# A graph network layer on one core: early phase reordered, node term by products, three VectorE operands moved to PSUM

## The chip, the cores and the metric

The kernel runs on one core of one Trainium2 chip. The metric is the device time of one execution in microseconds; the figure quoted is the median of six executions.

## The reference

There are 12,500 nodes with 96 features (`x`) and 412,500 directed edges, sorted by destination, with 4 attributes each. `_mlp` is a linear layer, ReLU and a normalisation over all rows (batch statistics).

```python
node_feat = _mlp(x, W_node, ...)                     # 12500 x 96
edge_feat = _mlp(edge_attr, W_edge, ...)             # 412500 x 96
message = _mlp(concat([x[row], x[col], edge_feat]), W_msg, ...)
agg = segment_sum(message, col, num_segments=12500)
out = layernorm(x + agg + node_feat)                 # per node, over 96 features
```

The batch normalisation of the messages is linear, so it can be applied after the segment sum; the kernel does so.

## The kernel before

**Tiling.** The edges are cut into tiles of 128, four tiles make a group (`GT`), four groups a block (`BG`): 806 groups, 202 blocks. As the edges are sorted, a block touches a short run of destination nodes; it starts at the node number `base[b]`.

**Tables.** `table` (line 144) multiplies all nodes by a 96x96 part of `W_msg` and writes the rows to DRAM, once for the source part (`p_tab`) and once for the destination part (`q_tab`). Its input `xp` is `x` transposed, loaded in seven pieces (line 98), on the queues of SP and ScalarE in turn. The tables' copies out of PSUM are shared by VectorE and ScalarE (lines 156, 158).

**Gathers.** Rows of `p_tab` are fetched for each tile of 128 edges by one indirect DMA that GpSimd issues (line 166). The first 26 blocks (the spilled ones; the first three of them take rows of `x` itself) are gathered ahead, during the early phase: `blocks` (line 171) gathers one block of 16 tiles into one of two `stage` buffers and writes it to DRAM (`spill`, line 177) from SP's queue. Each `next(store)` puts one such block into the program at that place: two during the first table, four during and after the second, three in `nodes`, the rest in `edge_norm`. The gathers stand in GpSimd's queue in block order and wait only for a free `stage` buffer, that is for the store two blocks before; the stores stand in SP's queue among its other DMAs, so a store can wait behind another DMA, and a DMA behind a store that waits for its gathers. After that, 28 groups are gathered into a ring (`pg`).

**Early phase, in order.** Tables; the check of the node windows (`rel`, line 209, subtracts the block's base node from every edge's destination; lines 213 to 223 reduce it to a flag); `places` (line 225: the same subtraction with edges in a linear layout, stored to DRAM as `rel_d`); `nodes` (line 245): `relu(x W_node + b)` into `agg`, its statistics, then on VectorE `xp = agg * a + xp` (line 260) and on ScalarE `xp = xp + c` (line 261) in ten pieces, then 98 products of `xp` with a centring matrix (line 266), which give `x + node_feat` less its mean over the features, copied (line 270) and stored (line 273) as `y0_d`; a memset of `agg`, which from there on is the sum per node; `edge_norm` (line 277): the edge layer for all edges, for its statistics alone: products (294), ReLU on ScalarE (298), `bn_stats` on VectorE (300).

**Main loop** (`fast`, from line 495, an order written out by hand for all engines, spilled blocks interleaved with the others: about one in eight). For each group `k`:

- `linear` (452): four products `z` of the edge features and one-hot places (`left`) with a matrix `rhs` that holds `w_e`, rows of `q_tab` and a bias. `z` has two buffers of one PSUM bank each, taken in turn.
- `message`: for even groups, `is_equal` (461) of `rel` against the constant `iota` gives the one-hot places of two groups in `h`; `hs = z + pg` (465), VectorE; `h = relu(hs)` (466), ScalarE.
- `sums` (477): `h` transposed times `h`, which gives sums per node and the statistics.
- per block, `edges` (437) makes the edge features of the next block; after group 2's message `prepare` writes them to `left`, half by ScalarE (444) and half by VectorE (445); `add` (490, 491) adds a block's sums.

In iteration `k` TensorE is given `linear(k+1)` and then `sums(k-1)`. When `hs(k)` is done, the ring slot of group `k` is free and GpSimd may gather the group that comes 28 later.

**Final phase** (from line 698): sums per node times a matrix made from the messages' normalisation, plus `y0_d`, layernorm, output.

Of the kernel before, what the change touches and what calls it, by code (L numbers as in the profile page):

```python
# [22 lines left out]
P = 128  # L23
# [53 lines left out]
def gnn(ctx, tc, t):  # L77
# [15 lines left out]
    ring = rpool.enter_context(tc.tile_pool(name="ring", bufs=RING))  # L93
    xp = xpool.enter_context(tc.tile_pool(name="x", bufs=1)).tile([C, XW], F32, name="xp")
    nc.scalar.dma_start(w_msg, t["L0_gnn_W_msg"].rearrange("(s k) f -> k s f", k=C))
    for i in range(0, NB, CH):
        part = slice(COL[i], COL[i + CH] if i + CH < NB else XW)
        (nc.scalar if i // CH % 2 else nc.sync).dma_start(xp[:, part], t["xp"][:, part])
    nc.scalar.dma_start(src, t["src"])

    ident = const.tile([P, P], F32, name="ident")
    make_identity(nc, ident)
# [12 lines left out]
    nc.vector.memset(step[:, 1, :], 1.0)  # L115
    nc.vector.memset(wide, 0.0)
    nc.vector.memset(we, 0.0)

    center = const.tile([C, C], F32, name="center")
# [3 lines left out]
    base = const.tile([1, NBL], I32, name="base")  # L123
    mstat = const.tile([C, 2], F32, name="mstat")
    vec = const.tile([C, len(_VECS)], F32, name="vec")
    v = {name[7:]: vec[:, i:i + 1] for i, name in enumerate(_VECS)}
# [66 lines left out]
    nc.sync.dma_start(base, t["base"])  # L193
# [9 lines left out]
    with tc.tile_pool(name="win", bufs=1) as win, tc.tile_pool(name="win_ps", bufs=2, space=PSUM) as ps:  # L203
        dsti = win.tile([P, NGP, GT], I32, name="dsti")
        nc.sync.dma_start(dsti, t["dst"].rearrange("p (g t) -> p g t", t=GT))
        basei = win.tile([P, NBL], I32, name="basei")
        nc.sync.dma_start(basei, t["base"].to_broadcast([P, NBL]))
        by_block = "p (b g) t -> p b (g t)"
        nc.vector.tensor_tensor(rel.rearrange(by_block, g=BG), dsti.rearrange(by_block, g=BG),
                                basei.unsqueeze(2).to_broadcast([P, NBL, BG * GT]), op=OP.subtract)  # L210
# [12 lines left out]
        nc.vector.tensor_scalar(flag, most, 0.0, None, op0=OP.is_gt)  # L223

    def places():

        with tc.tile_pool(name="lin", bufs=2) as work, tc.tile_pool(name="lin1", bufs=1) as one:
            first = one.tile([P, RW], I32, name="first")
            nc.sync.dma_start(first, t["first"])
            rows = rel_d.rearrange("o (p g e) -> (o p) g e", g=RW, e=GE)  # L230
            parts = [slice(i, min(i + 2, RW)) for i in range(0, RW, 2)]
            lins = []
            for i in range(len(parts) + 1):
                if i < len(parts):
                    n = parts[i].stop - parts[i].start
                    lins.append(work.tile([P, n, GE], I32, name="lin"))
                    nc.sync.dma_start(lins[i], t["dlin"][:, parts[i], :])
                    rlin = work.tile([P, n, GE], F32, name="rlin")
                    nc.vector.tensor_tensor(rlin, lins[i], first[:, parts[i]].unsqueeze(2).to_broadcast([P, n, GE]),
                                            op=OP.subtract)  # L240
                    lins[i] = rlin
                if i:
                    nc.sync.dma_start(rows[:, parts[i - 1], :], lins[i - 1])

    def nodes():

        with tc.tile_pool(name="nd", bufs=1) as one, tc.tile_pool(name="nd_ps", bufs=2, space=PSUM) as ps:
            stats = one.tile([C, -(-N // GE), 6], F32, name="nstats")
            for i, c in enumerate(range(0, N, GE)):
                n = min(GE, N - c)  # L250
                pn = ps.tile([C, GE], F32, name="pn", bufs=4)
                nc.tensor.matmul(pn[:, :n], w_node, xp[:, c:c + n], start=True, stop=True)
                nc.scalar.activation(agg[:C, c:c + n], pn[:, :n], AF.Relu, bias=v["b_node"], scale=1.0)
                nc.vector.bn_stats(stats[:, i, :], agg[:C, c:c + n])
            aggr = one.tile([C, 2], F32, name="naggr")
            nc.vector.bn_aggr(aggr, stats.rearrange("p a b -> p (a b)"))
            a_n, c_n = norm(aggr, v["g_node"], v["beta_node"], "node")
            for c in range(0, N, N // 10):
                x, y = agg[:C, c:c + N // 10], xp[:, c:c + N // 10]
                nc.vector.scalar_tensor_tensor(y, x, a_n, y, op0=OP.mult, op1=OP.add)  # L260
                nc.scalar.activation(y, y, AF.Identity, bias=c_n, scale=1.0)
            for i in range(0, NB, NBY):
                n = min(NBY, NB - i)
                py = ps.tile([P, 2, GE], F32, name="py0")
                for g in range(n):
                    nc.tensor.matmul(py[:, g // NBK, g % NBK * C:(g % NBK + 1) * C],
                                     xp[:, COL[i + g]:COL[i + g] + P], center, start=True, stop=True)
                y0 = one.tile([P, 2, NBK * C], F32, name="y0s", bufs=2)
# [62 lines left out]
    def fast(ring):  # L331
# [3 lines left out]
        with tc.manual_schedule(engines={ET.SP, ET.Pool}):  # L335
# [33 lines left out]
        with tc.tile_pool(name="fix", bufs=1) as fix, tc.tile_pool(name="msg", bufs=2) as work, \  # L369
# [85 lines left out]
            def message(k):  # L455
# [4 lines left out]
                if i % 2 == 0:  # L460
                    nc.vector.tensor_tensor(  # L461
                        h[:, :, :, C + 1:C + 1 + WN], rel[:, g:g + 2, :].unsqueeze(3).to_broadcast([P, 2, GT, WN]),
                        iota[:, i:i + 2, :].unsqueeze(2).to_broadcast([P, 2, GT, WN]), op=OP.is_equal)
                hs = work.tile([P, GT, C], F32, name="hs", bufs=3)
                nc.vector.tensor_add(hs[:, :n, :], z[:, :n, :], pg[:, :n, :])  # L465
                nc.scalar.activation(h[:, i % 2, :n, :C], hs[:, :n, :], AF.Relu)  # L466
# [229 lines left out]


    with tc.tile_pool(name="fin", bufs=2) as work, tc.tile_pool(name="fin_ps", bufs=2, space=PSUM) as ps:
        a_m, c_m = norm(mstat, v["g_msg"], v["beta_msg"], "msg")
        l = const.tile([C, C + 1], F32, name="l")  # L700
        nc.vector.tensor_scalar(l[:, :C], ident[:C, :C], a_m, None, op0=OP.mult)  # L701
        nc.vector.tensor_copy(l[:, C:C + 1], c_m)  # L702
        pd = ps.tile([C + 1, C], F32, name="pd", bufs=1)
        nc.tensor.matmul(pd, l, center, start=True, stop=True)  # L704
        d = const.tile([C + 1, C], F32, name="dm")
        nc.vector.tensor_copy(d, pd)  # L706

        out = t["out"]
        for i in range(0, NB, NBY):
# [58 lines left out]
```

## Time and profile before

| | |
|---|---|
| median of six executions | 5490.99 us (5481.06 to 5501.54) |
| profiled execution | 5504.1 us, span 5502.4 us |
| PE busy | 3509.8 us (64%), 16705 matmuls |
| PE weight loads busy | 2653.2 us (48%) |
| VectorE busy | 1717.5 us (31%) |
| ScalarE busy | 1132.7 us (21%) |
| GpSimd busy | 3053.4 us (55%) |
| mean granted TensorE clock | 0.667 |
| early phase (to the first message) | 0 to 1071.5 us |
| main loop | 1071.5 to 5436.6 us |
| final phase | 5436.6 to 5502.4 us |

No engine is busy for more than about two thirds of the span, so the time is in the waits between them. Matmul rows are issues whose ends are modelled: that a product is done is told by the start of the instruction that waits for it.

### The profile page before, as it was taken

To read this page: it belongs to the slowest core of one execution; us is meant where nothing else is said; L and a number is where in the kernel's file an instruction comes from. 1 tells how busy PE (TensorE), PEld (TensorE's weight loads), DVE (VectorE), ACT (ScalarE), POOL (GpSimd) and SP (SyncE) were. 2 spreads that over 40 slices of the span, in tenths; PEclk is the share of its full clock that TensorE was granted. 3 is DMA by queue.
4 is the path that set the end of the run, shared out by engine and by line. 5 is a ranking of instruction groups with operands and counts; after the bars stand their busy time and mean duration, and the time that the engine had idled before them with its cause. 6 is when DMAs were issued, how large, how long until landed. Compare 5 with 4: busy or idle time off the path is not lost. (4 is left out here: it accounts for less than half of the span.)

```text
span 5502.4 us, 48307 instructions
## 1 busy us (share of the span) xinstructions
PE 3509.8 (64%) x16705; PEld 2653.2 (48%) x16705; DVE 1717.5 (31%) x2837; ACT 1132.7 (21%) x1417; POOL 3053.4 (55%) x3231
## 2 busy tenths in 40 slices
PE   5556652666666666766665766766666666665677
PEld 5333320455555555545544555544444545555457
DVE  1345551722222222222222222222222222222235
ACT  0224441411111111111111111111111111111112
POOL 5454456155565555655566655666556666555650
PEclk9755555566666766666666666677667667666777
DMA  5332321111111111111111111111111111111112
GB/s 162 109 97 62 70 64 43 34 30 37 38 43 37 42 42 42 44 36 41 43 42 43 37 42 42 43 42 44 36 42 43 41 45 36 41 42 42 45 38 73
DMA packets 154615, 270.89 MB, mean 49 GB/s; under 512 B 83665, under 2 KB 84178, under 8 KB 153356
## 3 DMA queue, kind: packets, MB, share of 16 engines
q0 software_dynamic: 103136, 158.62, 12.0%
q1 hardware_dynamic: 48138, 98.39, 6.2%
q10 hardware_dynamic: 3088, 10.71, 0.6%
q8 instruction: 134, 2.20, 0.2%
q14 instruction: 119, 0.97, 0.1%
HBM read 225.88 MB, written 41.60 MB: 49 GB/s over the span
## 5 line engine op out<-in xcount | busy, mean ns | idle before, releaser
L166 POOL DMA_INDIRECT pg<-p_tab,src x2807 | 2656.6, 946 | 1893.5 <-DVE hs L465 1073.3
L452 PE MATMUL z<-rhs,left 128*128 128x96 f32 x6446 | 1232.4, 347 | 857.0 <-issue 701.8
L452 PEld LDWEIGHTS z<-rhs,left 128*128 128x128 f32 x6446 | 1115.0, 257 | 1182.1 <-issue 905.6
L477 PE MATMUL pa<-h 128*97 128x128 f32 x6446 | 1236.4, 335 | 462.2 <-issue 458.1
L477 PEld LDWEIGHTS pa<-h 128*97 128x97 f32 x6446 | 1032.1, 214 | 516.2 <-issue 515.1
L466 ACT ACTIVATE h<-hs 128x384 f32<-128x384 f32 x806 | 416.6, 523 | 3544.7 <-DVE hs L465 2452.8
L465 DVE TENSOR_TENSOR hs<-z,pg 128x384 f32<-128x384 f32 x702 | 383.1, 554 | 2402.1 <-remote 1304.2
L437 PE MATMUL pr<-ea,we 6*127 6x512 f32 x1404 | 542.7, 927 | 124.2 <-issue 110.3
L445 DVE TENSOR_SCALAR left<-pr 31x2048 f32<-31x2048 f32 x202 | 462.9, 2292 | 486.7 <-ACT left L444 258.7
L294 PE MATMUL pr<-ea,wide 10*128 10x512 f32 x1212 | 403.9, 1074 | 315.8 <-issue 214.2
L166 POOL DMA_INDIRECT stage<-p_tab,src x368 | 350.2, 952 | 381.2 <-DMA spill<-stage 248.3
L300 DVE BATCH_NORM_STATS2 estats<-r 128x6 f32<-128x512 f32 x606 | 365.4, 677 | 354.3 <-issue 227.4
L294 PEld LDWEIGHTS pr<-ea,wide 10*128 10x128 f32 x1212 | 202.5, 321 | 515.9 <-issue 333.2
L298 ACT ACTIVATE r<-pr 128x1024 f32<-128x1024 f32 x303 | 295.5, 1024 | 479.9 <-remote 342.2
L444 ACT ACTIVATE left<-pr 96x2048 f32<-96x2048 f32 x202 | 373.7, 1850 | 15.5 <-PE pr L437 15.5
L437 PEld LDWEIGHTS pr<-ea,we 6*127 6x127 f32 x1404 | 163.4, 254 | 341.5 <-issue 331.2
L461 DVE TENSOR_TENSOR h<-rel,iota 128x248 f32<-128x248 f32 x403 | 163.8, 407 | 0.0
L154 PE MATMUL pt<-w_msg,xp 96*128 96x96 f32 x392 | 88.5, 421 | 64.9 <-issue 35.7
L465 DVE TENSOR_TENSOR hs<-z,pb 128x384 f32<-128x384 f32 x104 | 57.1, 554 | 219.6 <-PE z L452 91.1
L154 PEld LDWEIGHTS pt<-w_msg,xp 96*128 96x128 f32 x392 | 85.3, 330 | 67.9 <-issue 47.8
L491 DVE TENSOR_TENSOR gram<-pa,gram 97x388 f32<-97x388 f32 x202 | 111.4, 551 | 0.0
L490 DVE TENSOR_TENSOR agg<-pa,agg 97x62 f32 x404 | 90.1, 223 | 14.1 <-PE pa L477 1.0
(106 smaller groups left out, 650.8 us busy)
## 6 DMA issues: line engine op xcount, KB each, us to landing
pg<-p_tab,src POOLq DMA_INDIRECT x2807
spill<-stage SPq DMA_DIRECT2D x26, 768.0 KB
pb<-spill SPq DMA_DIRECT2D x26, 768.0 KB
ea<-in_ea SPq DMA_DIRECT2D x75, 160.0 KB
rhs<-q_tab SPq DMA_DIRECT2D x404, 23.2 KB
ea<-in_ea SPq DMA_DIRECT2D x352, 20.0 KB
stage<-p_tab,src POOLq DMA_INDIRECT x368
q_tab<-trow SPq DMA_DIRECT2D x7, 672.0 KB
```

Of the source, the lines that this page charges most:

```text
L154: nc.tensor.matmul(pt[:, g, :], xp[:, k:k + P], w, start=True, stop=True)
L166: nc.gpsimd.indirect_dma_start(out=pg[:, i, :], out_offset=None, in_=tab[:, :], in_offset=bass.IndirectOffsetOnAxis(ap=idx[:, k:k + 1], ax ...
L294: nc.tensor.matmul(pr[:, k % 2, :], wide[Q * i:Q * i + 2 * EK, :], ea[Q * i:Q * i + 2 * EK, b % J, :], start=True, stop=True)
L298: nc.scalar.activation(r, pr, AF.Relu)
L300: nc.vector.bn_stats(stats[:, (k - o) % NS, (k - o) // NS, :], r[:, 1 - o, :])
L437: nc.tensor.matmul(prs[s][:C + WN, i, :], we[Q * i:Q * i + EK + 1, :], block[s][Q * i:Q * i + EK + 1, :], start=True, stop=True)
L444: nc.scalar.activation(x[:C, :n, :], pr[:C, :n, :], AF.Relu)
L445: nc.vector.tensor_scalar(x[C:C + WN, :n, :], pr[C:C + WN, :n, :], 0.0, None, op0=OP.is_equal)
L452: nc.tensor.matmul(zs[k][:, i, :], left[s % 2][:KR, g % BG, i * P:(i + 1) * P], rhs[:KR, s % RB, g % BG, :], start=True, stop=True)
L465: nc.vector.tensor_add(hs[:, :n, :], z[:, :n, :], pg[:, :n, :])
L466: nc.scalar.activation(h[:, i % 2, :n, :C], hs[:, :n, :], AF.Relu)
L477: nc.tensor.matmul(pas[s][:, g % BG, :C + 1 + WN], h[:r, i, :C + 1], h[:r, i, :C + 1 + WN], start=i == 0, stop=i == n - 1)
```

## The change

- **Loads in turn.** Four pieces of `xp` are loaded at first; each further piece is issued after a piece of the first table, on the queue of that table's store, and the load of the 1.6 MB index array `src` after the fourth. ScalarE's queue is put in program order for that stretch. `base` is loaded early.
- **Node features by products.** The scaling of lines 260 and 261 is gone. `a` and `c` go into a 97x96 matrix `d` (a diagonal and a row, times the centring matrix), and each tile of `y0` is the sum of two products in PSUM: `xp` with `center`, `agg` with `d`. `agg` has a row of ones for `c`, so it is set to 1 at the start; the memset to 0 at the end of `nodes` stays. Every second copy of `y0` goes to ScalarE. The final phase calls the same new function in place of its own lines.
- **Operands in PSUM.** The subtraction for `rel` takes the bases from PSUM (made there by a product with a row of ones; the broadcast load of 101 KB is gone); the one of `places` takes `first` from PSUM; `is_equal` takes its node numbers from a copy of `iota` in the unused end of the first of the two `z` banks. The two `z` buffers are now two fixed tiles.
- **Stores placed anew.** One more `next(store)` after `places`, and four in `nodes` (at its tiles 0, 3, 7, 11) instead of three (0, 4, 10).

```diff
-    for i in range(0, NB, CH):
+    def load_x(i):
         part = slice(COL[i], COL[i + CH] if i + CH < NB else XW)
         (nc.scalar if i // CH % 2 else nc.sync).dma_start(xp[:, part], t["xp"][:, part])
-    nc.scalar.dma_start(src, t["src"])
+    for i in range(0, 4 * CH, CH):
+        load_x(i)
...
+    nc.vector.memset(agg, 1.0)
...
+    def scaled(aggr, gamma, beta, name, ps):
+        a, c = norm(aggr, gamma, beta, name)
+        l = const.tile([C, C + 1], F32, name=f"l_{name}")
+        nc.vector.tensor_scalar(l[:, :C], ident[:C, :C], a, None, op0=OP.mult)
+        nc.vector.tensor_copy(l[:, C:C + 1], c)
+        nc.tensor.matmul(ps[:C + 1, :C], l, center, start=True, stop=True)
+        d = const.tile([C + 1, C], F32, name=f"d_{name}")
+        nc.vector.tensor_copy(d, ps[:C + 1, :C])
+        return d
...
-    with tc.manual_schedule(engines={ET.SP, ET.Pool}):
+    with tc.manual_schedule(engines={ET.SP, ET.Pool, ET.Activation}):
...
             for i, _ in enumerate(table(p_tab, ...)):
+                if (i + 4) * CH < NB:
+                    load_x((i + 4) * CH)
+                if i == 3:
+                    nc.scalar.dma_start(src, t["src"])
                 if i in (2, 5):
                     next(store)
...
-        nc.sync.dma_start(basei, t["base"].to_broadcast([P, NBL]))
+        nc.vector.tensor_copy(basef, base)
+        nc.tensor.matmul(pb, ones, basef, start=True, stop=True)
...
-                                basei.unsqueeze(2).to_broadcast([P, NBL, BG * GT]), op=OP.subtract)
+                                pb.unsqueeze(2).to_broadcast([P, NBL, BG * GT]), op=OP.subtract)
...
+            first = ps.tile([P, RW], F32, name="first")
+            nc.vector.tensor_copy(first, firsti)
...
-            a_n, c_n = norm(aggr, v["g_node"], v["beta_node"], "node")
-            for c in range(0, N, N // 10):
-                x, y = agg[:C, c:c + N // 10], xp[:, c:c + N // 10]
-                nc.vector.scalar_tensor_tensor(y, x, a_n, y, op0=OP.mult, op1=OP.add)
-                nc.scalar.activation(y, y, AF.Identity, bias=c_n, scale=1.0)
+            d = scaled(aggr, v["g_node"], v["beta_node"], "node", ps.tile([P, GE], F32, name="pn", bufs=4))
...
-                    nc.tensor.matmul(py[...], xp[:, COL[i + g]:COL[i + g] + P], center, start=True, stop=True)
+                    nc.tensor.matmul(to, xp[:, at], center, start=True, stop=False)
+                    nc.tensor.matmul(to, agg[:, at], d, start=False, stop=True)
...
-                if n == NBY:
+                if n == NBY and i // NBY % 2:
+                    nc.scalar.activation(y0, py[:, :, :NBK * C], AF.Copy)
+                elif n == NBY:
                     nc.vector.tensor_copy(y0, py[:, :, :NBK * C])
...
             places()
+            next(store)
             for i, _ in enumerate(nodes()):
-                if i in (0, 4, 10):
+                if i in (0, 3, 7, 11):
                     next(store)
...
+            zb = [ps.tile([P, GE], F32, name=f"z{i}", bufs=1) for i in range(2)]
+            nodes_of = zb[0][:, GT * C:GT * C + BG * WN].rearrange("p (k w) -> p k w", w=WN)
+            nc.vector.tensor_copy(nodes_of, iota)
...
-                zs[k] = ps.tile([P, GT, C], F32, name="z")
+                zs[k] = zb[k % 2][:, :GT * C].rearrange("p (t c) -> p t c", c=C)
...
-                        iota[:, i:i + 2, :].unsqueeze(2).to_broadcast([P, 2, GT, WN]), op=OP.is_equal)
+                        nodes_of[:, i:i + 2, :].unsqueeze(2).to_broadcast([P, 2, GT, WN]), op=OP.is_equal)
```

More of the change, by code (lines that the diff above doesn't have):

```diff
@@ L117, in gnn @@
     nc.vector.memset(we, 0.0)
+    ones = const.tile([1, P], F32, name="ones")
+    nc.vector.memset(ones, 1.0)
     center = const.tile([C, C], F32, name="center")
@@ L121, in gnn @@
     agg = const.tile([C + 1, WT], F32, name="agg")
+    nc.vector.memset(agg, 1.0)
     rel = const.tile([P, NGP, GT], F32, name="rel")
     base = const.tile([1, NBL], I32, name="base")
+    nc.sync.dma_start(base, t["base"])
     mstat = const.tile([C, 2], F32, name="mstat")
@@ L192, in gnn @@
     nc.sync.dma_start(b_msg, t["L0_gnn_b_msg"])
-    nc.sync.dma_start(base, t["base"])
     for i in range(NS):
@@ L205, in gnn @@
         nc.sync.dma_start(dsti, t["dst"].rearrange("p (g t) -> p g t", t=GT))
-        basei = win.tile([P, NBL], I32, name="basei")
-        nc.sync.dma_start(basei, t["base"].to_broadcast([P, NBL]))
+        basef = win.tile([1, NBL], F32, name="basef")
+        nc.vector.tensor_copy(basef, base)
+        pb = ps.tile([P, NBL], F32, name="pb", bufs=1)
+        nc.tensor.matmul(pb, ones, basef, start=True, stop=True)
         by_block = "p (b g) t -> p b (g t)"
         nc.vector.tensor_tensor(rel.rearrange(by_block, g=BG), dsti.rearrange(by_block, g=BG),
-                                basei.unsqueeze(2).to_broadcast([P, NBL, BG * GT]), op=OP.subtract)
+                                pb.unsqueeze(2).to_broadcast([P, NBL, BG * GT]), op=OP.subtract)
         worst = win.tile([P, 2, BG], F32, name="worst")
@@ L225, in places @@
     def places():
-        with tc.tile_pool(name="lin", bufs=2) as work, tc.tile_pool(name="lin1", bufs=1) as one:
-            first = one.tile([P, RW], I32, name="first")
-            nc.sync.dma_start(first, t["first"])
+        with tc.tile_pool(name="lin", bufs=2) as work, tc.tile_pool(name="lin1", bufs=1) as one, \
+                tc.tile_pool(name="lin_ps", bufs=1, space=PSUM) as ps:
+            firsti = one.tile([P, RW], I32, name="firsti")
+            nc.sync.dma_start(firsti, t["first"])
+            first = ps.tile([P, RW], F32, name="first")
+            nc.vector.tensor_copy(first, firsti)
             rows = rel_d.rearrange("o (p g e) -> (o p) g e", g=RW, e=GE)
@@ L245, in nodes @@
     def nodes():
-        with tc.tile_pool(name="nd", bufs=1) as one, tc.tile_pool(name="nd_ps", bufs=2, space=PSUM) as ps:
-            stats = one.tile([C, -(-N // GE), 6], F32, name="nstats")
+        with tc.tile_pool(name="nd", bufs=2) as one, tc.tile_pool(name="nd_ps", bufs=2, space=PSUM) as ps:
+            stats = one.tile([C, -(-N // GE), 6], F32, name="nstats", bufs=1)
             for i, c in enumerate(range(0, N, GE)):
                 n = min(GE, N - c)
-                pn = ps.tile([C, GE], F32, name="pn", bufs=4)
-                nc.tensor.matmul(pn[:, :n], w_node, xp[:, c:c + n], start=True, stop=True)
-                nc.scalar.activation(agg[:C, c:c + n], pn[:, :n], AF.Relu, bias=v["b_node"], scale=1.0)
+                pn = ps.tile([P, GE], F32, name="pn", bufs=4)
+                nc.tensor.matmul(pn[:C, :n], w_node, xp[:, c:c + n], start=True, stop=True)
+                nc.scalar.activation(agg[:C, c:c + n], pn[:C, :n], AF.Relu, bias=v["b_node"], scale=1.0)
                 nc.vector.bn_stats(stats[:, i, :], agg[:C, c:c + n])
-            aggr = one.tile([C, 2], F32, name="naggr")
+            aggr = one.tile([C, 2], F32, name="naggr", bufs=1)
             nc.vector.bn_aggr(aggr, stats.rearrange("p a b -> p (a b)"))
-            a_n, c_n = norm(aggr, v["g_node"], v["beta_node"], "node")
-            for c in range(0, N, N // 10):
-                x, y = agg[:C, c:c + N // 10], xp[:, c:c + N // 10]
-                nc.vector.scalar_tensor_tensor(y, x, a_n, y, op0=OP.mult, op1=OP.add)
-                nc.scalar.activation(y, y, AF.Identity, bias=c_n, scale=1.0)
+            d = scaled(aggr, v["g_node"], v["beta_node"], "node", ps.tile([P, GE], F32, name="pn", bufs=4))
             for i in range(0, NB, NBY):
@@ L265, in nodes @@
                 for g in range(n):
-                    nc.tensor.matmul(py[:, g // NBK, g % NBK * C:(g % NBK + 1) * C],
-                                     xp[:, COL[i + g]:COL[i + g] + P], center, start=True, stop=True)
-                y0 = one.tile([P, 2, NBK * C], F32, name="y0s", bufs=2)
-                if n == NBY:
+                    to, at = py[:, g // NBK, g % NBK * C:(g % NBK + 1) * C], slice(COL[i + g], COL[i + g] + P)
+                    nc.tensor.matmul(to, xp[:, at], center, start=True, stop=False)
+                    nc.tensor.matmul(to, agg[:, at], d, start=False, stop=True)
+                y0 = one.tile([P, 2, NBK * C], F32, name="y0s")
+                if n == NBY and i // NBY % 2:
+                    nc.scalar.activation(y0, py[:, :, :NBK * C], AF.Copy)
+                elif n == NBY:
                     nc.vector.tensor_copy(y0, py[:, :, :NBK * C])
@@ L698, in gnn @@
     with tc.tile_pool(name="fin", bufs=2) as work, tc.tile_pool(name="fin_ps", bufs=2, space=PSUM) as ps:
[L699 to L706, printed above, removed]
+        d = scaled(mstat, v["g_msg"], v["beta_msg"], "msg", ps.tile([C + 1, C], F32, name="pd", bufs=1))
         out = t["out"]
```

## The prediction

> **What bounds the kernel now.** The table of stages comes first (columns: window, its length, then busy us and instructions of PE, PE weight loads, VectorE, ScalarE, GpSimd; granted clock, DMA share, GB/s).
>
> ```profile
> 303.00:940.00 637.00, 338.69 (x996) 158.82 (x996) 297.34 (x498) 237.40 (x245) 347.19 (x368) 0.50 0.30 67
> 1071.50:5436.60 4365.10, 2883.89 (x14618) 2259.42 (x14617) 1201.51 (x2021) 776.40 (x1018) 2550.93 (x2695) 0.69 0.16 40
> ```
>
> The main loop holds 4365 of 5502 us and no engine fills it. So the bound is a chain, and it is read from a timeline of one ordinary block, VectorE first, then GpSimd.
>
> ```profile
> 2587.00 1.02 DVE L465 TENSOR_TENSOR hs<-z,pg 128x384 f32<-128x384 f32 x2 [12.59 <-remote]
> 2587.94 0.41 DVE L461 TENSOR_TENSOR h<-rel,iota 128x248 f32<-128x248 f32 x1
> 2591.09 0.56 DVE L465 TENSOR_TENSOR hs<-z,pg 128x384 f32<-128x384 f32 x1 [2.75 <-issue]
> 2594.00 2.30 DVE L445 TENSOR_SCALAR left<-pr 31x2048 f32<-31x2048 f32 x1 [2.35 <-issue]
> ...
> 2597.20 0.55 DVE L465 TENSOR_TENSOR hs<-z,pg 128x384 f32<-128x384 f32 x1
> 2597.66 0.41 DVE L461 TENSOR_TENSOR h<-rel,iota 128x248 f32<-128x248 f32 x1
> 2609.85 0.56 DVE L465 TENSOR_TENSOR hs<-z,pg 128x384 f32<-128x384 f32 x1 [11.78 <-PE pr L437]
> ```
>
> ```profile
> 2587.83 0.94 POOL L166 DMA_INDIRECT pg<-p_tab,src  x1 [3.85 <-DVE hs L465]
> 2589.07 0.94 POOL L166 DMA_INDIRECT pg<-p_tab,src  x1 [0.30 <-issue]
> ...
> 2597.81 1.08 POOL L166 DMA_INDIRECT pg<-p_tab,src  x1 [0.30 <-DVE hs L465]
> ...
> 2606.67 0.94 POOL L166 DMA_INDIRECT pg<-p_tab,src  x1 [0.30 <-issue]
> 2610.68 0.94 POOL L166 DMA_INDIRECT pg<-p_tab,src  x1 [3.06 <-DVE hs L465]
> ```
>
> Three things are to be seen. First, GpSimd gathers 16 tiles in a row (2587.83 to 2607.6, one per 1.247 us), then waits for the next block's group 0 (`hs` at 2609.85). Second, `is_equal` (L461) stands before `hs` of groups 0 and 2 and today runs in VectorE's idle time: at 2597.66, 12 us before `hs` of group 0 can start; at 2587.94, 3 us before group 2's. Third, after `hs` of group 2 (end 2591.65) come ScalarE's `h` (0.52) and `left` (1.85) and VectorE's `left` (2.30); only then does TensorE load the first weights of the next block's `z` (2596.37). Over all block boundaries that load starts 4.72 us after the end of group 2's `hs` (5th to 95th percentile 4.717 to 4.721): the boundary is a fixed latency.
>
> `hs` of group 0 waits 12 us for a product issued at 2596.4. Why TensorE is so slow there shows best in `edge_norm`, where ScalarE takes each finished pair of products at once:
>
> ```profile
> 818.77 1.02 ACT L298 ACTIVATE r<-pr 128x1024 f32<-128x1024 f32 x1 [10.18 <-remote]
> 829.97 1.02 ACT L298 ACTIVATE r<-pr 128x1024 f32<-128x1024 f32 x1 [10.18 <-remote]
> ...
> 965.40 3.02 ACT L298 ACTIVATE r<-pr 128x1024 f32<-128x1024 f32 x3 [0.25 <-ACT r L298]
> ```
>
> While GpSimd gathers (800 to 940) a pair takes 11.2 us; when it has stopped, about 1 us. All slow pairs lie in gather stretches, from some 8 us after a stretch begins to 2 us after it ends; the clock record says 0.50 throughout and doesn't show it. So gathering (35 blocks x 19.8 us = 693 us of the first 1071) and TensorE's work nearly take turns, in the early phase and in the loop.
>
> **The change, part by part.** The sum is made on the profiled execution, 5504.1 us (span 5502.4 and 1.7 around it), 13.1 us above the median of 5490.99.
>
> *is_equal in the bank of z.* Its operand now lies in the bank that TensorE writes with every even `z`. In the built program 400 of the 403 `is_equal` carry a wait for TensorE, where none had one; the `hs` behind it has lost its own. So `is_equal` waits for `z` of its group, and `hs` starts after it, not at once. Behind it queue `hs` of both groups, and behind those ScalarE's `h`, GpSimd (ring slot) and, for group 2, `left` and TensorE. Price of one: 0.41 us (row L461), of which 0.08 overlaps the next start (back to back, `hs` starts 0.33 after): 0.33 us.
>
> - Group 2: it enters the fixed latency. TensorE had finished group 3's `z` at 2593.73 (its semaphore) and had one group of `sums` left before it waited for `left`, so it idles there for about a microsecond and idles longer by the whole delay. 201 x 0.33 = **+66 us** (bounds 0, if TensorE is busy until then, and 201 x 0.41 = 82).
> - Group 0: it delays `hs`, and with it GpSimd in the 112 of 221 restarts that wait for group 0. But TensorE has a backlog at that moment and works fast until the gathers slow it, so what GpSimd starts late TensorE has done early. I take **0** (bounds 0 and 82).
> - Relief: `is_equal` read two SBUF operands, and the gather beside it took 1.08 us, not 0.94 (above); 72 gathers of the loop are so lengthened, by 0.12 each: **-8 us** (bounds -8 and 0, as GpSimd is not what a block always waits for).
>
> Reading from PSUM is not dearer: 388 elements with one PSUM operand (`gram`) take 551 ns, or 404 ns of elements and 147 fixed; `is_equal`, 258 and 148.
>
> Two rules of the Trainium skill bear on this. "SBUF — State Buffer", section "Who interferes with whom", says that a VectorE instruction with two SBUF inputs contends with a GpSimd instruction that reads SBUF, and that the second to issue is blocked fully. The trace agrees at `rel`:
>
> ```profile
> 96.66 3.53 DVE L209 TENSOR_TENSOR rel<-dsti,basei 128x3232 f32<-128x3232 int32 x1 [11.34 <-DMA dsti<-in_dst]
> 97.75 3.25 POOL L166 DMA_INDIRECT stage<-p_tab,src  x1 [0.30 <-issue]
> ```
>
> By that rule alone each `is_equal` could block a gather for its 0.41 us and the change could save up to 165 us; the rows give 8. "PSUM — Partial Sum Buffer", section "PSUM bank collisions raise a hardware error", speaks against: accesses of two engines must be kept apart by bank, not by address. By it the 400 waits can't be dropped; the trace of before shows no such pair.
>
> *Early phase.* (1) `y0`: 98 more products of two issues each. Row L266 has 196 issues in 44.0 us, so **+44 us** (bounds: 0 where they fall into a gather's slow stretch that was idle, about 137 us if all run at the 0.70 us an issue seen there at 140 to 166 us). (2) L260 and L261 ran as one chain from 231.2 to 246.4; `l`, one product and `d` take about 1 us like the same lines of the final phase: **-14 us**. (3) First table: SP's first store of it is issued at 33.70, behind small loads that wait for the big ones, and TensorE stalls for the row buffers from 30.5 to 33.2 and 37.8 to 38.6, and then runs into the slow stretch at 45; with fewer loads in flight the store comes up to 12 us earlier, and gathers from `p_tab` start that much before 90.3: **-11 us** (bounds -22, all of GpSimd's wait from 68.7 to 90.3, and +10, if later pieces of `xp`, queued behind stores on SP and ScalarE, come late). (4) Stores: GpSimd idles from 216.8 to 252.3 because store 6 stands behind `y0`'s first store in SP's queue. Placed after `places`, it lets a block of 19.8 us into that hole; but the last ten products of `nodes`, which ran fast there (221 to 230), become slow. Of 0 to 20 I take **-13 us**; the other blocks move with `y0` at no gain. SP is moved past nothing else that waits. (5) The memset of `agg` (10.6 us, row L275) ran during `y0`; now it must wait for the last `y0` product and stands ahead of the first `bn_stats` of `edge_norm`: **+10 us** (bounds 0, if a slow stretch covers it, and 11). The second memset, at the start, delays only the first copy (11.63 us) by about 1. (6) Half the `y0` copies on ScalarE, `rel` and `first` from PSUM: **0**; six copies of 0.95 us lie beside products, `rel` frees the one gather of 3.25 us (-2 at most), the additions are below a microsecond each and lie beside table work.
>
> Early sum: 44 - 14 - 11 - 13 + 10 = **+16 us**. Whole: 66 + 0 - 8 + 16 = **+74 us**: 5578 us for a profiled execution, 5565 us against the median.
>
> **Rivals.** *A, faster:* TensorE's backlog covers the wait of group 2 too (0), and the early phase gets its full gains: store hole -20, table -22, scaling -14, memset +10, the added products covered by slow stretches (0), relief -8: -54, or 5437. It decides if the exposed wait is below about 0.1 us a block. For it: TensorE is behind in half of all blocks (`hs` of group 0 waits for it 12 us). Against it: the constant 4.72 us at the boundary. *B, both waits exposed in full:* 403 x 0.41 = 165, with +16 - 8: 5664. For it: `hs` of group 0 ends GpSimd's longest waits. Against: TensorE's work per block does not grow. *C, no difference:* the wait is hidden and the early parts cancel: 5491 within 11 us. It needs two coincidences. That the change doesn't do what it says has no place: the built program shows each part.
>
> **Numbers.** Own case 0.57 (alone 5515 to 5620), A 0.22, B 0.13, C 0.08. The measurement tells 0.2% (11 us) from no change. Faster 0.24 (A and a little of the own case's lower end), same 0.08, slower 0.68. The range 5437 to 5640 leaves out half of A and the greater part of B, about 0.19.
>
> **What would show it.** In the profile after: `is_equal` no longer 12 us ahead of `hs` but directly before it, with an idle time ended by PE; a block boundary still at 4.72 us from `hs`, and the loop longer by 50 to 80 us; gathers of 1.05 us and more gone; the first gather from `p_tab` before 85 us; the first message at 1075 to 1105 us. I am wrong if the loop is not longer (A, C), if it grows by over 130 us (B), or if the added `y0` products cost the early phase over 60 us or nothing.

## The result and the profile after

The changed kernel takes **5534.6 us** (median; 5519.0 to 5542.1), the kernel before, timed beside it, 5501.9 us (5477.1 to 5516.9): ratio **1.006, 95% interval 1.005 to 1.0069**, or 33 us slower (27 to 38). The forecast was +74 us, 5565 against the median of the first runs, with slower at 0.68. The sign came out as told, and so did the total of the early phase; the loop did not.

The table of stages of the profiled execution after (5530.5 us, span 5528.7; columns: window, its length, then busy us and instructions of PE, PE weight loads, VectorE, ScalarE, GpSimd; granted clock, DMA share, GB/s):

```profile
0.00:1092.60 1092.60, 611.35 (x2078) 384.35 (x2079) 470.08 (x735) 333.53 (x367) 499.39 (x536) 0.60 0.30 79
1092.60:5462.70 4370.10, 2698.63 (x14616) 2213.15 (x14615) 1207.77 (x2022) 779.62 (x1018) 2542.34 (x2695) 0.70 0.16 40
```

The early phase is 21 us longer than before (forecast 16), the loop only 5 us (forecast 58). The wait itself is there as forecast. This is an ordinary block after, VectorE's timeline:

```profile
2600.29 0.56 DVE L496 TENSOR_TENSOR hs<-z,pg 128x384 f32<-128x384 f32 x1 [10.42 <-remote]
2600.76 0.40 DVE L492 TENSOR_TENSOR h<-rel,z 128x248 f32<-128x248 f32 x1
2601.08 0.55 DVE L496 TENSOR_TENSOR hs<-z,pg 128x384 f32<-128x384 f32 x1
2602.96 0.56 DVE L496 TENSOR_TENSOR hs<-z,pg 128x384 f32<-128x384 f32 x1 [1.32 <-PE z L483]
2608.64 0.41 DVE L492 TENSOR_TENSOR h<-rel,z 128x248 f32<-128x248 f32 x1 [5.12 <-issue]
2608.97 0.55 DVE L496 TENSOR_TENSOR hs<-z,pg 128x384 f32<-128x384 f32 x1
2611.93 2.30 DVE L476 TENSOR_SCALAR left<-pr 31x2048 f32<-31x2048 f32 x1 [2.41 <-ACT left L475]
...
2623.94 0.56 DVE L496 TENSOR_TENSOR hs<-z,pg 128x384 f32<-128x384 f32 x1 [8.73 <-remote]
```

Each `is_equal` (L492) now stands directly before its `hs`: the `hs` starts 0.32 to 0.33 us after it, in groups 0 (2601.08) and 2 (2608.97), and in 395 of the 403 cases `is_equal` ends 0.08 us after the start of that `hs`. Of the 1254.5 us for which VectorE sat idle before `is_equal`, 343.3 ended with TensorE's `z`, as its group's row says:

```profile
L492 DVE TENSOR_TENSOR h<-rel,z 128x248 f32<-128x248 f32 x403 | 164.8, 409 | 1254.5 <-remote 363.1 <-PE z L483 343.3 <-issue 342.6
```

The boundary (end of group 2's `hs` to TensorE's next `z`) is 4.76 us, from 4.72. Yet the median ordinary block takes 23.64 us, where it took 23.65. GpSimd's timeline of the same block says why:

```profile
2601.12 0.94 POOL L184 DMA_INDIRECT pg<-p_tab,src  x1 [3.91 <-DVE hs L496]
2602.36 0.94 POOL L184 DMA_INDIRECT pg<-p_tab,src  x1 [0.30 <-issue]
...
2619.84 0.94 POOL L184 DMA_INDIRECT pg<-p_tab,src  x1 [0.30 <-issue]
2624.77 0.94 POOL L184 DMA_INDIRECT pg<-p_tab,src  x1 [3.99 <-DVE hs L496]
```

From one restart to the next 23.65 us pass: 16 gathers (19.66) and a pause of 3.99. The `hs` that ends the pause starts at 2623.94, 3.2 us after the last gather's end (2620.78); before, 2.2 us (2609.85 after 2607.6, in group 0). Over the loop the median of this distance is 3.15 us after and 3.02 before, and 128 of 209 runs of gathers are 16 long (124 of 221 before); what moved is the `hs` that ends the pause, group 0's in 112 of 221 cases before, group 3's in 137 of 209 after. Group 2's `is_equal` (2608.64) lies in the middle of the gathers, where TensorE is slow; as I read these rows, what it holds up there is waited for only when the gathers have stopped.

### The profile page after: what moved, and what is told of

It reads as the page before. It is cut to its first block, busy times and chain, and to the rows that moved or that the text cites. A ratio compares the mean times of both kernels' runs of the same rounds, so it can differ in the third digit from the quotient of the medians.

```text
span 5528.7 us, 48668 instructions
## 1 busy us (share of the span) xinstructions
PE 3360.5 (61%) x16905; PEld 2647.4 (48%) x16905; DVE 1716.3 (31%) x2829; ACT 1127.9 (20%) x1413; POOL 3041.7 (55%) x3231
## 5 line engine op out<-in xcount | busy, mean ns | idle before, releaser
L483 PE MATMUL z<-rhs,left 128*128 128x96 f32 x6446 | 1247.0, 353 | 1243.6 <-DVE hs L496 524.9
L508 PE MATMUL pa<-h 128*97 128x128 f32 x6446 | 1225.2, 339 | 354.8 <-issue 353.6
L508 PEld LDWEIGHTS pa<-h 128*97 128x97 f32 x6446 | 1050.9, 219 | 351.8 <-issue 350.8
L319 PE MATMUL pr<-ea,wide 10*128 10x512 f32 x1212 | 396.8, 1075 | 294.2 <-issue 177.1
L492 DVE TENSOR_TENSOR h<-rel,z 128x248 f32<-128x248 f32 x403 | 164.8, 409 | 1254.5 <-remote 363.1
L468 PE MATMUL pr<-ea,we 6*127 6x512 f32 x1404 | 358.0, 882 | 48.9 <-issue 36.6
L468 PEld LDWEIGHTS pr<-ea,we 6*127 6x127 f32 x1404 | 97.2, 244 | 144.3 <-issue 134.0
```

Of the source, the lines that this page charges most:

```text
L319: nc.tensor.matmul(pr[:, k % 2, :], wide[Q * i:Q * i + 2 * EK, :], ea[Q * i:Q * i + 2 * EK, b % J, :], start=True, stop=True)
L468: nc.tensor.matmul(prs[s][:C + WN, i, :], we[Q * i:Q * i + EK + 1, :], block[s][Q * i:Q * i + EK + 1, :], start=True, stop=True)
L508: nc.tensor.matmul(pas[s][:, g % BG, :C + 1 + WN], h[:r, i, :C + 1], h[:r, i, :C + 1 + WN], start=i == 0, stop=i == n - 1)
```

## The experiments

All ratios are to the kernel before measured beside it, with a 95% interval; a microsecond figure is the ratio times the median of before. The kernel before was timed anew with each of four groups of runs: in three it took 5445 to 5447 us, in one 4139 (the four runs told of as "at 4139 us"); results of the two kinds are kept apart. Each profile is of one execution. The expectations name two theories: 'covered' (an ordinary block hides the wait) and 'given back' (the wait costs 66 us there, and the operand in PSUM returns as much).

**1. The loop's part alone** (before, with node numbers in the end of `z`'s first bank).

```diff
+            nodes_of = zb[0][:, GT * C:GT * C + BG * WN]...
...
-                zs[k] = ps.tile([P, GT, C], F32, name="z")
+                zs[k] = zb[k % 2][:, :GT * C].rearrange("p (t c) -> p t c", c=C)
...
-                        iota[:, i:i + 2, :]...
+                        nodes_of[:, i:i + 2, :]...
```

> Before, with only the main loop's part of the change: node numbers in the end of the first z bank, is_equal waits for z. Theory 'covered': the wait costs nothing in the 175 ordinary blocks and about 0.75 us in each of the 26 spilled ones (19 us); with the relief of the lengthened gathers (-9 us) the loop grows by 5 to 15 us, the whole kernel by 0.1 to 0.3%. Rival 'given back': the same total, so this run only says whether the loop's part is as small alone as it was in the whole change.

Measured: 1.0032 (1.0021 to 1.0044), +17 us (11 to 24). No gather of the loop is above 0.97 us (72 before). So the loop's part is slower, at the upper end of what was expected of this run (0.1 to 0.3%), but by less than a third of the 58 us forecast.

**2. The early part alone** (the changed kernel with `iota` back in SBUF for `is_equal`).

> The changed kernel with is_equal reading iota in SBUF again, so the early phase's part alone. Both theories: the first message at 1085 to 1100 us as in the changed kernel, the loop back at 4355 to 4370 us, 15 to 30 us above before (0.3 to 0.5%).

Measured: 1.0045 (1.003 to 1.006), +24 us (16 to 33). The loop takes 4318.9 us and the first message comes at 1072.9, both earlier than expected; the kernel before itself was 57 us faster in this group of runs than beside the changed kernel (5445 and 5502). With run 1 that makes 42 us, against 33 (27 to 38) for the whole: the two parts add up within their intervals.

**3. The wait alone** (before, operands in SBUF, a one-element copy of `z` ahead of `is_equal`).

```diff
+                    nc.vector.tensor_copy(look, z[:, 0, :1])
                     nc.vector.tensor_tensor(
                         h[:, :, :, C + 1:C + 1 + WN], ...
```

> Before, with a copy of one element of z ahead of each is_equal, so that is_equal waits for z while its operands stay in SBUF: the wait without the relief. Theory 'covered': ordinary blocks as before (23.6 us median, 4030 us in all), spilled blocks 0.75 to 1.1 us longer each (20 to 28 us), kernel +0.3 to 0.6%. Rival 'given back' (the wait costs 66 us in ordinary blocks and the PSUM operand returns as much): loop +85 to 120 us, kernel +1.5 to 2.2%.

Measured: 1.0049 (1.0034 to 1.0065), +27 us (19 to 35). The wait, put on without the change of memory, costs as much as the loop's part or a little more; the copy is an instruction of its own. That is inside 'covered' (0.3 to 0.6%) and far below 'given back' (1.5 to 2.2%).

**4. PSUM without the wait** (before, with the numbers in the end of the *other* `z` bank, and `is_equal` issued ahead of the next `linear`).

```diff
+            nodes_of = zb[1][:, GT * C:GT * C + BG * WN]...
...
+                    if k < n:
+                        onehot(k)
```

> Before, with the node numbers in the end of the second z bank and is_equal issued ahead of the next linear, so that it waits for no product of its own group: the relief without the wait. Theory 'covered': relief of 8 us, spilled blocks as before, kernel -0.3% to 0. Rival 'given back': ordinary blocks 60 to 80 us shorter in all, kernel -1.0 to -1.5%.

Measured: 0.9991 (0.9976 to 1.0006). The long gathers are gone (0), the total is -5 us (-13 to +3). 'Given back' had -1.0 to -1.5% here, so it falls with this run and run 3. So the relief of the gathers is small, and runs 1 and 4 differ by the wait: 0.41%, some 22 us, or 0.11 us a block. The loops of the profiled executions fall into two sets in this state: 4340.1 and 4348.7 us with the wait (runs 1 and 3), 4314.9 to 4327.9 without (runs 2, 4, 9, 10, 11, 12).

**5 and 6. The wait where no gather covers it** (at 4139 us). Run 5 is before with the loop's gathers left out, so that its sums are of other rows, run 6 the same with the loop's part of the change.

```diff
+            kept = dict(got)
...
-                        got[ahead] = ahead_of(ahead)
+                        got[ahead] = kept[SPILL + (ahead - SPILL) % RING]
```

> Before, without the main loop's gathers (the ring of 28 groups is filled once and used again, so the sums are of other rows); all else in the loop is issued as before. Theory 'covered' (an ordinary block is set by GpSimd's gathers and the slow TensorE beside them): a block falls from 23.6 to the 12 or 13 us of a spilled block, the loop from 4365 to about 2500 us. Rival (the block is a chain of latencies on TensorE, VectorE and ScalarE, gathers beside it): the loop stays above 4000 us.

> The same with is_equal's node numbers in the bank of z, so with the wait. Theory 'covered': without gathers nothing covers the wait, so each block shows both is_equals, 0.65 to 0.75 us: loop 130 to 150 us above the run without gathers and without the wait. Rival: 0 to 20 us, as beside the gathers.

Measured: 3221.1 and 3344.9 us, one execution each. The stage rows of the main loops, run 5 and then run 6:

```profile
650.80:3153.40 2502.60, 1931.26 (x14616) 1706.28 (x14616) 1192.50 (x2021) 781.58 (x1018) 35.85 (x38) 0.91 0.06 18
```

```profile
654.70:3277.40 2622.70, 1996.41 (x14616) 1765.81 (x14616) 1196.58 (x2022) 781.48 (x1018) 35.36 (x38) 0.89 0.06 17
```

Without gathers the loop takes 2503 us, as 'covered' said (about 2500). Its rival's mark of 4000 us is no test here, since at 4139 us the loop takes 3388 with the gathers too (run 8). With the wait it grows by 120 us (130 to 150 expected), 0.59 us a block: nearly both waits (2 x 0.33), and 5 times the 0.11 us of runs 1 and 4. VectorE's timelines show it, in run 5 with `is_equal` 2.6 us ahead of group 2's `hs`, in run 6 directly before it, released by TensorE:

```profile
2007.48 0.41 DVE L462 TENSOR_TENSOR h<-rel,iota 128x248 f32<-128x248 f32 x1
2010.09 0.56 DVE L466 TENSOR_TENSOR hs<-z,pg 128x384 f32<-128x384 f32 x1 [2.20 <-PE z L453]
2013.00 2.30 DVE L446 TENSOR_SCALAR left<-pr 31x2048 f32<-31x2048 f32 x1 [2.35 <-ACT left L445]
```

```profile
2003.64 0.41 DVE L466 TENSOR_TENSOR h<-rel,z 128x248 f32<-128x248 f32 x1 [2.50 <-PE z L457]
2003.97 0.55 DVE L470 TENSOR_TENSOR hs<-z,pg 128x384 f32<-128x384 f32 x1
2006.93 2.30 DVE L450 TENSOR_SCALAR left<-pr 31x2048 f32<-31x2048 f32 x1 [2.41 <-ACT left L449]
```

So the price of the wait was right, and four fifths of it do not show beside the gathers of runs 1 and 4. These differ from runs 5 and 6 in a second way, in that TensorE is slow there (see the last section); the wait beside gathers at 4139 us was not run.

**7. The node features by products alone** (before, with the second product of `y0`, the memset and `scaled`; at 4139 us).

> Before, with the node features by products alone (98 more products, agg's row of ones and its later memset, no scaling, half the copies on ScalarE). Forecast's terms: +44 -14 +10 = +40 us, first message at 1085 to 1120 us. Rival (the products fall into slow stretches that were idle): 0 to +10 us.

Measured: 1.0067 (1.005 to 1.0083), +28 us (21 to 34), against 44 - 14 + 10 = 40 forecast; the rival (0 to +10) is out. The first message comes at 685.4 us, in run 8 at 681.1. The two totals lie 26 us apart all the same, because at 4139 us the gathers set the pace: once the early phase is over, GpSimd never pauses in run 7 and for 5 us in all in run 8. So what counts here is what holds up the gathers. With `y0` longer, the stores of gathered blocks stand longer behind the stores of `y0` in SP's queue, and GpSimd pauses for 12.4, 7.2, 21.3 and 8.8 us between 172 and 282 us, 49.7 in all. In run 5, whose early phase is that of before, it pauses once there, for 18.0. The longest pause of run 7, then that of run 5:

```profile
253.01 0.94 POOL L179 DMA_INDIRECT stage<-p_tab,src  x1 [21.31 <-DMA spill<-stage]
```

```profile
190.56 0.94 POOL L166 DMA_INDIRECT stage<-p_tab,src  x1 [17.98 <-DMA spill<-stage]
```

**8 and 9. The stores anew alone**, first at 4139 us, then at 5446.

```diff
             places()
+            next(store)
             for i, _ in enumerate(nodes()):
-                if i in (0, 4, 10):
+                if i in (0, 3, 7, 11):
```

> Before, with the stores of gathered blocks placed anew alone. Forecast's term: -13 us (0 to -20). Rival (the hole is filled, but TensorE's products of nodes become slow and later holes grow): 0 to +10 us.

> The kernel before with the five later stores of the early phase placed as in the changed kernel, and nothing else. Theory (stores): on a chip where the early gathers slow TensorE's products (edge products with a pitch above 6 us, as in the profile before), the stores alone bring most of what the kernel with loads and stores cost (ratio 1.0034): +15 to +25 us (ratio 1.003 to 1.005), with the early gathers ended some 8 us earlier than before (near 914 to 932 us), and 155 to 162 us instead of 130 to 132 us from there to the first message. Rival (loads): the stores cost nothing here (ratio 0.999 to 1.001), and the stretch from the last early gather to the first message stays below 135 us. On a chip without slow products both expect what the first run of it gave, 1.000.

Measured: 1.0003 (0.9994 to 1.0013) at 4139 us; 1.0019 (1.0004 to 1.0034), +10 us (2 to 19), at 5446. No gain in either. Run 8 does not have the pause of 18.0 us that run 5 shows, and is no faster; why, no run shows. At 5446 us the early gathers end at 912.9 us, and it takes 158.2 us from there to the first message, both about as the theory said; the cost is below the 15 us that it gave as least. VectorE's timeline of `nodes` in this run, in the changed kernel, and the end of the statistics in the kernel before:

```profile
207.83 0.69 DVE L254 BATCH_NORM_STATS2 nstats<-agg 96x6 f32<-96x512 f32 x1 [0.69 <-ACT agg L253]
212.73 0.69 DVE L254 BATCH_NORM_STATS2 nstats<-agg 96x6 f32<-96x512 f32 x1 [4.21 <-ACT agg L253]
218.33 0.69 DVE L254 BATCH_NORM_STATS2 nstats<-agg 96x6 f32<-96x512 f32 x1 [4.91 <-issue]
...
242.44 0.83 DVE L256 BATCH_NORM_AGGREGATE naggr<-nstats 96x2 f32<-96x150 f32 x1
```

```profile
204.38 0.69 DVE L280 BATCH_NORM_STATS2 nstats<-agg 96x6 f32<-96x512 f32 x1 [1.22 <-ACT agg L279]
209.30 0.69 DVE L280 BATCH_NORM_STATS2 nstats<-agg 96x6 f32<-96x512 f32 x1 [4.23 <-ACT agg L279]
214.93 0.69 DVE L280 BATCH_NORM_STATS2 nstats<-agg 96x6 f32<-96x512 f32 x1 [4.94 <-ACT agg L279]
...
251.21 0.83 DVE L282 BATCH_NORM_AGGREGATE naggr<-nstats 96x2 f32<-96x150 f32 x1
```

```profile
230.36 0.83 DVE L256 BATCH_NORM_AGGREGATE naggr<-nstats 96x2 f32<-96x150 f32 x1
```

Block 8 of the gathers now runs right after block 7, in the changed kernel from 213.1 to 232.8 us, in the hole that was idle before. Beside it one `nodes` product takes 5.6 us. There the statistics end at 251.2 (before: 230.4), and all that follows on TensorE starts later. GpSimd is done with its early gathers 8 us sooner (932.2, from 939.9), and TensorE needs 160.4 us from there to the first message, from 131.6.

**10. Loads and stores together** (the changed kernel with the old scaling and `iota` in SBUF; `rel` and `places` keep their PSUM operands).

> The changed kernel with the old scaling and with is_equal reading iota in SBUF: loads in turn, stores placed anew and the PSUM operands of rel and places alone. Forecast's terms: -11 - 13 - 2 = -26 us. Theory after the first runs (early part +24 as a whole, products +27): -5 to 0 us, first message within 5 us of before.

Measured: 1.0034 (1.0017 to 1.005), +18 us (9 to 27). This was expected at -5 to 0, so the miss was in what I held to be gains.

**11. The same with is_equal of run 4**, meant as the best version.

> The changed kernel with the old scaling of the node features and with is_equal's node numbers in the second z bank, issued ahead of the next linear (no wait). Theory (the products cost about 27 us, the wait 18 to 27, the relief 7, the rest of the early phase about -3): 5 to 15 us below before, -0.1 to -0.3%. Rival (loads and stores cost as well): at or above before.

Measured: 1.0036 (1.0021 to 1.005), +20 us (11 to 27). The expectation failed with that of run 10. The two share the loads and stores, and the gathers end at 914.6 us here, with 158.2 from there to the first message.

**12. Loads in turn, and is_equal of run 4, with the old places of the stores.**

> The kernel before with two parts of the change: the loads in turn, and is_equal with its node numbers in PSUM, here in the other z buffer and issued ahead of the next linear, so that it doesn't wait for the product. Stores and node features are those of before. Theory (stores cost, the rest doesn't): -5 to -15 us (ratio 0.997 to 0.999), the first message 0 to 8 us earlier than in the kernel before, the stretch from the last early gather to the first message 130 to 132 us on a chip with slow products. Rival (loads cost): +10 us or more (ratio above 1.002), with the first message at least 10 us later.

Measured: 5428.2 us against 5446.6, 0.9978 (0.9959 to 0.9996), -12 us (-22 to -2), as expected: **a little faster than before**, though only just clear of it, and by these ratios faster than the changed kernel, which was not timed beside it. The first message comes at 1041.0 us, earlier than expected: in runs 1, 3 and 4, which share its old store places, at 1053.1 to 1058.8. From the last early gather to it 130.9 us pass. Its row of the `nodes` statistics, and that of run 9 (name, count, durations, first and last start):

```profile
L260 DVE BATCH_NORM_STATS2 nstats<-agg x25: 359/672/690, 194.5 to 208.8; 96x6 f32<-96x512 f32 x24, 96x6 f32<-96x212 f32 x1
```

```profile
L254 DVE BATCH_NORM_STATS2 nstats<-agg x25: 359/673/691, 197.6 to 242.0; 96x6 f32<-96x512 f32 x24, 96x6 f32<-96x212 f32 x1
```

In run 12 they are over at 209, before block 8 starts (231.1): the hole, which the prediction took for waste, let `nodes` run fast.

## Why the prediction was right or wrong

The forecast of slower held, with about the right early total and a loop that was three times too dear. The early total is luck: 16 us were forecast, 21 (profiles) to 24 (run 2) measured, but at 5446 us the products cost 34 us less than forecast, the stores 23 us more, and the loads gained less or nothing, and these errors cancel. Term by term, in us:

| term | forecast | runs |
|---|---|---|
| the wait, groups 2 and 0 | +66 + 0 | +22 (run 1 less 4), +27 (run 3) |
| relief of the gathers | -8 | -5 (run 4) |
| products, less scaling, plus memset | +40 | +28 at 4139 us (run 7); about +6 at 5446 (run 2 less 10) |
| stores | -13 | +10 at 5446, +1 at 4139 (runs 9, 8) |
| loads | -11 | about -7 with old stores (run 12 less 4), no gain with the new (run 10 less 9, with the PSUM operands of `rel` and `places`: +8) |
| sum | +74 | whole change measured: +33 (27 to 38); the rows at 5446 us add up to 26 to 46 |

Differences between two runs carry the uncertainty of both, some 10 us, and those of 2 and 10, 12 and 4, and 10 and 9 were not measured side by side.

**Step that failed: group 2's wait.** The chain was right: `is_equal` waits, stands directly before `hs`, and group 2's lies at the boundary, at a price near 0.33 us (0.59 for both groups, runs 5 and 6). Its term was mis-sized, at +66 where the runs show +22 to +27 for both groups together, by the reading that the boundary's latency sets the block: "it idles there for about a microsecond and idles longer by the whole delay". But most often an ordinary block is 16 gathers and a pause, ended by an `hs` that starts some 3 us after the last of them. The prediction had used this very argument for group 0 ("works fast until the gathers slow it") and did not apply it to group 2. That the 0.11 us a block that remain are what TensorE loses in the slow stretch is argued, not shown; nor did the runs settle in which blocks they fall. In the two profiled executions the 175 ordinary blocks take 4016.6 us after and 4030.9 before, and the 26 spilled ones 351.9 and 332.6; but run 4 has 354.8 there without the wait, so this is no proof that the spilled blocks pay. Run 1 against run 4 even speaks for the ordinary blocks (3980.6 and 3964.4 us, the spilled ones 358.0 and 354.8), against the expectation of run 1. The profiles before and after alone would give the loop +5 us; by the ratios it is +17.

**Relief.** The size was right. By the Trainium skill's rule in "SBUF — State Buffer", section "Who interferes with whom", the change could have saved up to 165 us, as the prediction estimated. Run 4 takes the contention away wholly (72 long gathers to 0) and gains 5 us, with no change at all inside its interval. The operand in PSUM is not dearer, as the prediction said: `is_equal` takes 402 ns on average in run 4, 407 before.

**The bank rule.** The prediction named the Trainium skill's "PSUM — Partial Sum Buffer", section "PSUM bank collisions raise a hardware error", which keeps two engines apart by bank, as speaking against. Run 4 shows a way round that the prediction did not see: with the numbers in the other bank, and issued ahead of the product that writes that bank, `is_equal` no longer waits for its own group's product. In run 12 it again ends 2.75 us (median) ahead of its `hs`, as in run 9, which has `iota` in SBUF.

**Products.** The stretch of `y0` grew as told: 246.4 to 303.1 before, 260.5 to 364.5 after, +47 us (forecast 44). The rows of both products after (of 196 issues each, 62.0 us busy; before, one row of 196 with 44.0):

```profile
L290 PE MATMUL py<-d_node,agg 97*128 97x96 f32 x196 | 62.0, 418 | 6.0 <-issue 5.6 <-DVE d_node L158 0.3
L289 PE MATMUL py<-center,xp 96*128 96x96 f32 x196 | 62.0, 414 | 5.9 <-issue 5.9
```

But `edge_norm`, which follows, shrank from 710 to 669 us: it has 35 slow intervals between pairs of products (320 us), where it had 40 (372 us), as more of the gather stretches lay beside `y0`. The bound of 0 in the prediction, not its middle, was nearest at 5446 us. The +28 us of run 7 came another way, through GpSimd's pauses.

**Stores.** The prediction gave the reason against itself ("the last ten products of `nodes`, which ran fast there (221 to 230), become slow") and counted it lower than the 20 us gained. It is the larger: in the changed kernel GpSimd is done 8 us sooner, and TensorE takes 29 us more behind it.

**Loads.** SP's first store to the table came at 20.0 us, from 33.7, as forecast. The first gather from the table came at 87.5, from 90.3: forecast before 85, missed. For SP's second store to the table came later, at 49.2, from 36.5, and behind it stand a load and the first spill store. SP's timeline after, then before:

```profile
20.04 0.38 SPq L177 DMA_DIRECT2D p_tab<-trow  x1
20.47 0.66 SPq L99 DMA_DIRECT2D xp<-in_xp  x1
49.16 0.34 SPq L177 DMA_DIRECT2D p_tab<-trow  x1
49.55 0.43 SPq L99 DMA_DIRECT2D xp<-in_xp  x1
50.29 1.01 SPq L195 DMA_DIRECT2D spill<-stage  x1
```

```profile
33.70 0.53 SPq L159 DMA_DIRECT2D p_tab<-trow  x1
...
36.49 0.35 SPq L159 DMA_DIRECT2D p_tab<-trow  x1
38.12 0.71 SPq L177 DMA_DIRECT2D spill<-stage  x1
```

The spill went out at 38.1 us before, at 50.3 now, so the third block's gathers start at 59.7, from 49.0. That is the bad end the prediction gave for this term ("later pieces of `xp`, queued behind stores on SP and ScalarE, come late"), though through the spill and not through `xp`; why the second store is late, no run shows.

**The rest of the list.** `is_equal` directly before `hs`, with idle time ended by PE (right); boundary 4.76 us (4.72, right but for 0.04); gathers above 1.05 us gone (right); first message at 1092.6 (1075 to 1105, right); loop longer by 50 to 80 (wrong). Of early gathers the prediction counted 35 blocks; the profile has 33 (26 spilled, 7 for the ring), and nothing in its sum rests on that. Rival A came near in the loop, where it put the exposed wait below about 0.1 us a block and runs 1 and 4 give 0.11, but its early gains were not there: stores and products cost. Rival B (165 us for both waits) is near what runs 5 and 6 show where nothing covers them (120).

## What to carry to other kernels

A fixed latency in the trace is not yet the bound: ask whether what it delays is waited for at once, or only when a longer stretch beside it is over, and apply the answer to every wait in the block alike. A hole in one engine's work may be the time in which another runs fast; before it is filled, find out whose pace it sets. An operand in a bank that another engine writes cost nothing that could be measured where its reader was issued before that write (run 4), and a wait where it was issued behind it (run 1).

## What the runs showed of the hardware that was not expected

**TensorE is slow beside GpSimd's gathers, and not always.** In the profile after, one pair of edge products takes 11.2 us beside gathers and 1.14 without (ScalarE's timeline; a row may stand for several, back to back):

```profile
813.74 1.02 ACT L323 ACTIVATE r<-pr 128x1024 f32<-128x1024 f32 x1 [10.19 <-remote]
824.94 1.02 ACT L323 ACTIVATE r<-pr 128x1024 f32<-128x1024 f32 x1 [10.18 <-remote]
...
957.63 2.86 ACT L323 ACTIVATE r<-pr 128x1024 f32<-128x1024 f32 x3 [0.25 <-ACT r L323]
961.05 2.86 ACT L323 ACTIVATE r<-pr 128x1024 f32<-128x1024 f32 x3 [0.56 <-DVE estats L325]
```

GpSimd's timeline beside the first of these pairs:

```profile
812.68 0.94 POOL L184 DMA_INDIRECT pg<-p_tab,src  x1 [0.30 <-issue]
813.93 0.94 POOL L184 DMA_INDIRECT pg<-p_tab,src  x1 [0.30 <-issue]
```

The slowness outlasts the gathers by more than the 2 us that the prediction read: the last slow pair ends at 947.1 us, 15 us after the last early gather (932.2), and before at 959.0, 19 us after it (939.9).

In run 8, at 4139 us, the same gathers at the same pitch leave it at 1.14 us, three pairs in 3.41. First ScalarE's timeline, then GpSimd's:

```profile
403.02 2.85 ACT L298 ACTIVATE r<-pr 128x1024 f32<-128x1024 f32 x3 [0.56 <-ACT r L298]
406.43 2.85 ACT L298 ACTIVATE r<-pr 128x1024 f32<-128x1024 f32 x3 [0.56 <-ACT r L298]
```

```profile
403.68 0.94 POOL L166 DMA_INDIRECT stage<-p_tab,src  x1 [0.30 <-issue]
404.93 0.95 POOL L166 DMA_INDIRECT stage<-p_tab,src  x1 [0.30 <-issue]
```

The granted clock is 0.50 in both stretches, and so doesn't tell them apart. Of the 302 intervals between pairs 35 are above 6 us in the profile after (320 us in all), 4 in run 8 (26 us) and none in run 7. What in the gathers slows TensorE stays open, and as the ends of products are modelled, the rows can't tell a slow product from a late signal of its end. Whether it is the chip or a state of it stays open too; the record gives the runs at 4139 us and runs 9 to 12, at 5446, the same chip number, 6, which speaks for a state. It also goes with what parts of a change are worth: the stores cost 10 us with it and nothing without, and the products some 6 with it and 28 without.
